# Recurrent layers of a four-stage block: the short convolution moved off TensorE, the clip folded into a product, output scalings gathered on ScalarE

## The chip, the cores and the metric

One core of a Trainium2 chip runs the whole program in one launch. The metric is the device time of one execution in microseconds (us), from runs on the chip. Engines are called as in the profile: PE (TensorE, matmul), PEld (its weight loads), DVE (VectorE), ACT (ScalarE), POOL (GpSimd), SP (SyncE).

## The reference

The block takes x of shape 8 x 512 x 256 in float32 and applies four sublayers, each followed by a residual addition and a layer norm: three gated recurrent layers, an expert layer in which experts choose tokens, an attention layer, and an expert layer in which tokens choose experts. The change lies in the recurrent layers alone:

```python
def _rglru_layer(x, cw, cb, wrw, wrb, wiw, wib, la, wow, nw):
    xp = jnp.pad(x, ((0, 0), (KCONV - 1, 0), (0, 0)))             # KCONV = 4
    x_conv = cb + sum((xp[:, k:k + Lx, :] * cw[:, k] for k in range(KCONV)))
    r_t = jax.nn.sigmoid(x_conv @ wrw.T + wrb)
    i_t = jax.nn.sigmoid(x_conv @ wiw.T + wib)
    a_base = jax.nn.sigmoid(la.astype(jnp.float32)).astype(x.dtype)
    a_t = a_base ** (8.0 * r_t)
    b_t = jnp.sqrt(jnp.clip(1.0 - a_t * a_t, 1e-06, None)) * (i_t * x_conv)
    h = _parallel_scan(a_t, b_t)
    return _rmsnorm(h @ wow.T, nw)
...
for l in range(NLAYERS):                                          # NLAYERS = 3
    h = _rglru_layer(h, conv_w[l], ...)
return _rmsnorm(h, norm_out_w)
```

## The kernel before

The 4096 tokens are cut into four groups of two sequences (1024 tokens). A *unit* u is one layer on one group: three layers times four groups make U = 12 units, u = 0 to 11, with the group index changing fastest. Channels lie on the 128 partitions, in two chunks (`dc` = 0, 1), and tokens along the free dimension, so a tile of a unit is 128 x 2 x 2 x 512 elements (chunk, sequence, time).

The work of a unit is software-pipelined over rounds t = -2 to 11. In round t the kernel convolves unit t+2 (`conv`, `taps`), forms the gates of unit t+1 (`gate`, `square_decay`), does the scans of unit t (`sums`, `decay`, `clip`, `root`, `gated`, `inputs`, `scan`), and projects, normalizes and transposes back unit t-1 (`project`, `norm`, `scaled`, `turn`). Rounds -2 to 8 are written in `usual`, rounds 9 to 11 in `late` (unit t-1 is then one of the last layer), and `end` finishes the last unit. PE, ACT and DVE run under a manual schedule: each executes its instructions in exactly the order in which these functions issue them. So an instruction that waits holds back all that was issued behind it on its engine.

The steps that the change and the prediction speak of:

- `conv(u, i)` (L252) starts the convolution. Where `on_pe(u, dc)` holds, PE multiplies with two diagonal matrices (L268 and L271, the tap of shift 0 and that of shift 1, half a chunk at a time) and ACT moves the sum from PSUM to the tile `xc` with the bias (L274). Elsewhere ACT forms the tap of shift 0 with the bias for a whole chunk at once (L261). Before, `on_pe` holds for chunk 0 of every unit and for both chunks of the last unit.
- `taps(u, dc)` (L278) adds the other shifts on DVE (L283): shifts 2 and 3 where PE took part, shifts 1, 2 and 3 elsewhere.
- `gate` (L288): PE multiplies `xc` with the two gate matrices (L296), ACT applies a tanh (L300) and writes `R` and `I`. `square_decay` (L304): ACT writes Q, the squared decay, from R.
- `sums(u, dc)` (L313) on DVE: a bounded sum of logarithms by scans, then differences, into `D`. `decay` (L329): ACT takes the exponential of `D`. `clip` (L335) on DVE turns Q into min(Q - 1, -1e-6). `root` (L339): ACT takes the square root of -Q/4. `gated` (L342) and `inputs` (L345) on DVE multiply I with `xc` and with that root; `scan` (L348) runs the recurrence on DVE into `h`, of which there is one buffer.
- `project` (L357): PE multiplies h with the output matrix (L369) into PSUM, ACT squares and sums each 256 wide row (L379). In the last layer DVE first multiplies by a weight (L375). `norm` (L394): a square root on ACT (L400, or L405 in the last layer), a reciprocal on DVE (L407). `scaled(u, c)` (L409) scales each of eight pieces: in the first two layers ACT does six (L418) and DVE those with c = 2 and 3 (L416), from PSUM into Y. `turn` (L420) transposes Y back on PE, and ACT writes `xT` (L430).

ACT's functions need tables: root and norm use another table than the exponentials and the tanh, so each round has two table loads. All PSUM tiles of these layers come from one pool of eight banks, in which a new tile takes the bank whose last use stands earliest in program order.

In a usual round ACT's order is: squares of two projections, `decay` of chunk 0, convolution, squares of the other two, table load, `root`, `norm`, `scaled`, table load, `decay` of chunk 1, R, Q, then I and `xT` in turn. DVE's order is: sums of chunk 0, `clip`, sums of chunk 1, `gated`, first tap of chunk 1, reciprocal, the other taps of chunk 1, `scaled`, `inputs`, taps of chunk 0, four scans.

Of the kernel before, what the change touches and what calls it, by code (L numbers as in the profile page):

```python
# [10 lines left out]
F32 = mybir.dt.float32  # L11
I32 = mybir.dt.int32
AF = mybir.ActivationFunctionType
ALU = mybir.AluOpType
# [3 lines left out]
P = 128  # L18
# [132 lines left out]
def recurrent_layers(tc, x_tok, xT, lg, ident, eps6, eps5, acc, kept, a):  # L151
# [5 lines left out]
    nc = tc.nc  # L157
# [4 lines left out]
    U = NL * NG  # L162
    with ExitStack() as ctx:
        wp = ctx.enter_context(tc.tile_pool(name="rw", reuse_waits="tile", bufs=1))
# [29 lines left out]
        nc.vector.memset(wg, 0.0)  # L194
        nc.scalar.dma_start(wg[:, :, :E0], a["Wg"].rearrange("(dc p) e -> p dc e", p=P))

        on_pe = lambda u, dc: dc == 0 or u == U - 1
        diag = {}
        for l in range(NL):
            for dc in range(DC):  # L200
# [17 lines left out]
        table = wp.tile([P, 1], F32, name="table")  # L218
        one = wp.tile([P, 1], F32, name="one1")
        nc.vector.memset(one, 1.0)  # L220
        eps12 = wp.tile([P, 1], F32, name="eps12")
        nc.vector.memset(eps12, RMS_EPS * RMS_EPS)

# [26 lines left out]
        xcs, Rs, Is, Qs, Cs, Ds, hs, Ys, ws, sss = ({} for _ in range(10))  # L250

        def conv(u, i):  # L252


            l, q = stages[u]
            dc, b = divmod(i, NB)
            if i == 0:
                xcs[u] = new("xc", u, 3)
            if not on_pe(u, dc):
                if b == 0:  # L260
                    nc.scalar.activation(  # L261
                        xcs[u][:, dc].rearrange("p b t -> p (b t)"), xT[:, dc, q * W : (q + 1) * W],
                        AF.Identity, bias=par[:, l, dc, CB : CB + 1], scale=par[:, l, dc, 3:4],
                    )
                return
            ps = psG.tile([P, S], F32, tag="g", name=f"conv_{u}_{i}")
            at = q * W + b * S
            nc.tensor.matmul(  # L268
                ps, diag[l, dc, 0], xT[:, dc, at : at + S], start=True, stop=False
            )  # L270
            nc.tensor.matmul(  # L271
                ps[:, 1:], diag[l, dc, 1], xT[:, dc, at : at + S - 1], start=False, stop=True
            )
            nc.scalar.activation(  # L274
                xcs[u][:, dc, b, :], ps, AF.Identity, bias=par[:, l, dc, CB : CB + 1]
            )

        def taps(u, dc, k=slice(None)):  # L278
            l, q = stages[u]
            src = xT[:, dc, q * W : (q + 1) * W].rearrange("p (b t) -> p b t", b=NB)  # L280
            dst = xcs[u][:, dc]
            for s in ((2, 3) if on_pe(u, dc) else (1, 2, 3))[k]:
                nc.vector.scalar_tensor_tensor(  # L283
                    dst[:, :, s:], src[:, :, : S - s], par[:, l, dc, 3 - s : 4 - s],
                    dst[:, :, s:], ALU.mult, ALU.add,
                )
# [26 lines left out]
        def sums(u, dc):  # L313

            l, q = stages[u]
            if dc == 0:
                Cs[u], Ds[u] = new("C", u, 1), new("D", u, 1)
            C, Df = Cs[u][:, dc], Ds[u][:, dc]
            nc.vector.tensor_scalar(
                Df, Rs[u][:, dc], 1.0, mlim[:, l, dc : dc + 1], ALU.add, ALU.min  # L320
            )
            for b in range(NB):
                nc.vector.tensor_tensor_scan(
                    C[:, b, :], Df[:, b, :], clim[:, l, dc : dc + 1].to_broadcast([P, S]),
                    0.0, ALU.add, ALU.min,
                )
            nc.vector.tensor_sub(Df[:, :, 1:], C[:, :, 1:], C[:, :, : S - 1])

        def decay(u, dc):  # L329
            l, q = stages[u]  # L330
            nc.scalar.activation(
                Ds[u][:, dc], Ds[u][:, dc], AF.Exp, scale=neg4[:, l, dc : dc + 1]
            )

        def clip(u):  # L335

            nc.vector.tensor_scalar(Qs[u], Qs[u], 1.0, -1e-6, ALU.subtract, ALU.min)

        def root(u):  # L339
            nc.scalar.activation(Qs[u], Qs[u], AF.Sqrt, scale=-0.25)  # L340

        def gated(u):  # L342
            nc.vector.scalar_tensor_tensor(Is[u], Is[u], 1.0, xcs[u], ALU.add, ALU.mult)

        def inputs(u):  # L345
            nc.vector.tensor_mul(Is[u], Is[u], Qs[u])

        def scan(u, dc):  # L348
            if dc == 0:
# [44 lines left out]
        def norm(u, c0=0, n=NCH, last=False):  # L394


            l, q = stages[u]
            s = sss[u][:, 0, c0 : c0 + n]
            if l < NL - 1:
                nc.scalar.activation(s, s, AF.Sqrt, bias=eps6, scale=1.0 / D)  # L400
            else:
                nc.vector.scalar_tensor_tensor(
                    s, s, RMS_EPS, sss[u][:, 1, c0 : c0 + n], ALU.mult, ALU.add
                )
                nc.scalar.activation(s, s, AF.Sqrt, bias=eps12, scale=1.0 / D)  # L405
            if not last:
                nc.vector.reciprocal(s, s)  # L407

        def scaled(u, c):  # L409
            l, q = stages[u]  # L410
            s = sss[u][:, 0, c : c + 1]
            dst, src = Ys[u][:, c, :], ws[u][c // 2][:, c % 2, :]
            if l == NL - 1:
                nc.vector.scalar_tensor_tensor(dst, dst, s, nob, ALU.mult, ALU.mult)
            elif c // 2 == 1:
                nc.vector.tensor_scalar_mul(dst, src, s)  # L416
            else:
                nc.scalar.mul(dst, src, s)  # L418

# [27 lines left out]
        def last_norm(u, c0, n):  # L447

            last_root(u, c0, n)
            last_scale(u, c0, n)  # L450
            last_apply(u, c0, n)
# [90 lines left out]
        def usual(t):  # L542
            A, G, R, O, N = on(t + 2), on(t + 1), on(t), on(t - 1), is_last(t - 2)
            if R:
                sums(t, 0)
                clip(t)
                sums(t, 1)
                gated(t)
            for i in range(4):
                if O:  # L550
                    project(t - 1, i)
                if R and i == 1:
                    decay(t, 0)
                if A and i == 1:
                    conv(t + 2, 0)
                    conv(t + 2, 2)
            if A:
                taps(t + 2, 1, slice(0, 1))
            if R:
                root(t)  # L560
            if O:
                norm(t - 1)
            if A:
                taps(t + 2, 1, slice(1, 3))
            if O:
                for c in range(NCH):
                    scaled(t - 1, c)
            if R:
                inputs(t)
            if A:  # L570
                conv(t + 2, 1)
                taps(t + 2, 0)
            if R:
                decay(t, 1)
                scan(t, 0)
                scan(t, 1)
            for i in range(4):
                if G:
                    gate(t + 1, 0, i)
            if G:  # L580
                square_decay(t + 1)
            for i in range(4):
                if G:
                    gate(t + 1, 1, i)
                if O:
                    turn(t - 1, i)

        def late(t):


            A, G, N = on(t + 2), on(t + 1), is_last(t - 2)
            sums(t, 0)
            for i in range(4):
                project(t - 1, i)
                if i == 1:
                    decay(t, 0)
                    if A:
                        conv(t + 2, 0)
                    clip(t)
            if is_last(t - 3):  # L600
                for b in range(NB):
                    logits(t - 3, b)
                take_logits(t - 3)
            sums(t, 1)
            decay(t, 1)
            gated(t)
            root(t)
            norm(t - 1)
            if N:
                last_norm(t - 2, 0, NCH)  # L610
                keep(t - 2, 0, NCH)
            inputs(t)
            if A:
                for i in range(1, 4):
                    conv(t + 2, i)
                taps(t + 2, 0)
            scan(t, 0)
            if A:
                taps(t + 2, 1)
            scan(t, 1)  # L620
            for c in range(NCH):
                scaled(t - 1, c)
            if G:
                for i in range(4):
                    gate(t + 1, 0, i)
                square_decay(t + 1)
            for b in range(NB):
                residual(t - 1, b)
            for i in range(4):
                if G:  # L630
                    gate(t + 1, 1, i)
                if N:
                    last_turn(t - 2, i)
# [50 lines left out]
        for t in range(-2, U):  # L684
            (late if is_last(t - 1) else usual)(t)
# [1610 lines left out]
```

## Time and profile before

| what | value |
|---|---|
| median of 3 runs | 1828.58 us (1828.22 to 1832.04) |
| profiled execution, its own time | 1832.25 us |
| its span in the profile | 1830.5 us |
| mean granted TensorE clock | 0.968 of full |
| busy: PE, DVE, ACT, POOL | 1683.4, 1135.8, 972.1, 510.8 us |
| first sums of round 1 start at | 58.08 us |
| eight rounds, 1 to 8 | 58.08 to 265.50 us |
| three late rounds, 9 to 11 | 265.50 to 369.6 us |
| end of the recurrent layers and last logits | to about 403 us |
| everything else | 403 to 1830.5 us |

Times inside the program are from the span's start. "Busy" adds up an engine's instructions, of which neighbours may overlap by about 0.1 us; the ends of matmuls are modelled. A line number is that of the kernel before unless the text says otherwise. A line of the timeline gives start, duration, engine, source line, operation, output <- inputs, shapes and count; the bracket says how long the engine was idle before and whose result ended the idle time. The stretches are cut at the first DVE instruction of a round (L319).

### The profile page before, as it was taken

To read this page: it belongs to the slowest core of one execution; us is meant where nothing else is said; L and a number is where in the kernel's file an instruction comes from. 1 tells how busy PE (TensorE), PEld (TensorE's weight loads), DVE (VectorE), ACT (ScalarE), POOL (GpSimd) and SP (SyncE) were. 2 spreads that over 40 slices of the span, in tenths; PEclk is the share of its full clock that TensorE was granted. 3 is DMA by queue.
4 is the path that set the end of the run, shared out by engine and by line. 5 is a ranking of instruction groups with operands and counts; after the bars stand their busy time and mean duration, and the time that the engine had idled before them with its cause. 6 is when DMAs were issued, how large, how long until landed. Compare 5 with 4: busy or idle time off the path is not lost. (4 is left out here: it accounts for less than half of the span.)

```text
span 1830.5 us, 31418 instructions
## 1 busy us (share of the span) xinstructions
PE 1683.4 (92%) x10280; PEld 1104.9 (60%) x10280; DVE 1135.8 (62%) x2846; ACT 972.1 (53%) x2128; POOL 510.8 (28%) x464
## 2 busy tenths in 40 slices
PE   6999997567999799999999999988999999999995
PEld 2555663346999575222222232226999889999984
DVE  5999998787222644687978888785453222222227
ACT  4899986631232423566666665656454343343333
POOL 1000000000554410010242341424667644444440
PEclk8999999679999899999999999999999999999998
DMA  9200000032451400000011120125766678575548
GB/s 356 75 1 0 1 1 1 23 127 102 125 169 59 121 6 7 18 18 16 27 57 40 40 68 18 62 78 162 176 161 146 145 193 218 102 166 119 98 90 265
DMA packets 108424, 167.30 MB, mean 91 GB/s; under 512 B 16669, under 2 KB 83807, under 8 KB 108000
## 3 DMA queue, kind: packets, MB, share of 16 engines
q1 hardware_dynamic: 76064, 117.74, 20.3%
q0 software_dynamic: 29184, 44.85, 12.7%
q10 hardware_dynamic: 3008, 2.63, 0.4%
q8 instruction: 86, 1.41, 0.3%
q14 instruction: 82, 0.67, 0.1%
HBM read 232.75 MB, written 60.07 MB: 160 GB/s over the span
## 5 line engine op out<-in xcount | busy, mean ns | idle before, releaser
L2053 DVE TENSOR_REDUCE nmx<-s 128x1 f32<-128x512 f32 x512 | 329.8, 686 | 100.9 <-PE t L1972 76.7
L2060 ACT ACTIVATE pe<-t 128x512 f32<-128x512 f32 x512 | 277.5, 595 | 187.5 <-PE t L1972 178.4
L1957 PE MATMUL s<-kT,qT 32*128 32x512 f32 x1024 | 289.5, 640 | 24.4 <-DVE nmx L2053 13.8
L1972 PE MATMUL t<-qA,kT 32*128 32x512 f32 x1024 | 285.1, 641 | 0.3 <-DVE nmx L2053 0.3
L2149 POOL DMA_INDIRECT acc<-y,at x136 | 211.4, 1554 | 240.8 <-DVE at L2142 165.0
L1957 PEld LDWEIGHTS s<-kT,qT 32*128 32x128 f32 x1024 | 78.7, 183 | 171.7 <-ACT pe L2060 158.3
L972 ACT ACTIVATE m1hT<-m1h,m1ws 128x128 f32<-128x128 f32 x272 | 99.3, 368 | 152.1 <-PE m1h L966 114.2
L2148 DVE TENSOR_SCALAR y<-m1o,gt 128x256 f32<-128x256 f32 x136 | 65.8, 484 | 174.4 <-PE m1o L988 163.9
L972 ACT ACTIVATE m1hT<-m1h,xT 128x128 f32<-128x128 f32 x272 | 98.5, 368 | 135.3 <-PE m1h L966 103.3
L955 DVE COPY m1xq<-m1xp 128x256 f32<-128x256 f32 x136 | 57.7, 424 | 168.2 <-PE m1h L966 108.0
L735 POOL DMA_INDIRECT m1rows<-x_ext,slot x128 | 128.4, 1003 | 97.6 <-ACT pe L2060 64.1
L1996 PE MATMUL po<-pe,V 128*17 128x512 f32 x1024 | 135.1, 600 | 1.4 <-ACT pe L2060 1.0
L966 PEld LDWEIGHTS m1h<-m1xq,m1ws 128*128 128x128 f32 x1088 | 133.0, 194 | 3.7 <-issue 0.5
L966 PE MATMUL m1h<-m1xq,m1ws 128*128 128x128 f32 x1088 | 134.5, 277 | 0.0
L966 PEld LDWEIGHTS m1h<-m1xq,xT 128*128 128x128 f32 x1088 | 131.5, 192 | 4.8 <-DVE m1xq L955 0.9
L966 PE MATMUL m1h<-m1xq,xT 128*128 128x128 f32 x1088 | 132.9, 275 | 0.8 <-DVE m1xq L955 0.7
L988 PE MATMUL m1o<-m1ws,m1hT 128*128 128x256 f32 x544 | 129.3, 381 | 0.6 <-issue 0.6
L988 PE MATMUL m1o<-xT,m1hT 128*128 128x256 f32 x544 | 128.7, 379 | 0.0
L2026 POOL TENSOR_TENSOR AO<-AO,on 128x256 f32<-128x256 f32 x32 | 23.6, 737 | 349.2 <-DVE on L2021 235.6
L988 PEld LDWEIGHTS m1o<-m1ws,m1hT 128*128 128x128 f32 x544 | 98.6, 191 | 11.6 <-issue 1.0
L988 PEld LDWEIGHTS m1o<-xT,m1hT 128*128 128x128 f32 x544 | 98.1, 190 | 10.5
L296 PE MATMUL gate<-xc,wi 128*128 128x512 f32 x192 | 92.1, 611 | 2.5 <-ACT junk L379 2.5
(367 smaller groups left out, 2925.3 us busy)
## 6 DMA issues: line engine op xcount, KB each, us to landing
m1ws<-in_w_pack SPq DMA_DIRECT2D x68, 522.0 KB
m1ws<-in_w_pack SPq DMA_DIRECT2D x68, 512.0 KB
xT<-in_w_pack SPq DMA_DIRECT2D x66, 522.0 KB
xT<-in_w_pack SPq DMA_DIRECT2D x66, 512.0 KB
m0ws<-in_w_pack SPq DMA_DIRECT2D x36, 522.0 KB
m1xg<-m1rows SPq DMA_DIRECT2D x136, 138.0 KB
m0ws<-in_w_pack SPq DMA_DIRECT2D x36, 512.0 KB
acc<-zero SPq DMA_DIRECT2D x2, 4096.0 KB
```

The source lines that it names most:

```text
L296: nc.tensor.matmul(ps, w[("wr", "wi")[g]][:, l, dc, oc * P : (oc + 1) * P], xcs[u][:, dc, b, :], start=(dc == 0), stop=(dc == DC - 1),)
L735: ins = self.nc.gpsimd.indirect_dma_start(out=self.rows[:, :], out_offset=bass.IndirectOffsetOnAxis(ap=place, axis=0), in_=row, in_offset= ...
L966: nc.tensor.matmul(ps, w[:, o : o + P], xq[:, dc, :], start=(dc == 0), stop=(dc == DC - 1),)
L972: ins = nc.scalar.activation(hT[:, fc, :], ps, AF.Gelu, bias=w[:, o : o + 1])
L988: nc.tensor.matmul(ps, hT[:, fc, :], w[:, o : o + D], start=(fc == 0), stop=(fc == FC - 1))
L1957: mm = nc.tensor.matmul(ps, qTs[u % NR][r, qc * P : (qc + 1) * P], kTs[u % NR][r, :], start=True, stop=True,)
L1972: mm = nc.tensor.matmul(ps, kTs[v % NR][r, kc * P : (kc + 1) * P], qAs[v][r, :], start=True, stop=True,)
L1996: mm = nc.tensor.matmul(po[h4 * HP : h4 * HP + VW, :], V[:, b * NQ + kc, 4 * g + h4, :], pes.pop((u, kc, h4)), start=(kc == 0), stop=(kc = ...
L2053: ins = nc.vector.tensor_reduce(at, ps, AX.X, ALU.max, negate=True)
L2060: ins = nc.scalar.activation(pe, ps, AF.Exp)
L2148: nc.vector.tensor_scalar_mul(y, ps, gt)
L2149: nc.gpsimd.indirect_dma_start(out=R.acc[t % 2][:, :], out_offset=bass.IndirectOffsetOnAxis(ap=at, axis=0), in_=y, in_offset=None, compute ...
```

## The change

Three edits. First, `on_pe` holds for the last unit only: in the eleven units before it ACT forms the first tap of both chunks, one instruction for each, and DVE adds three shifts for both. Half of the diagonal matrices are no longer built on POOL (L205), since only those of the last layer are used. Second, `clip` is gone: the root takes sqrt(1/4 + 2^-24 - Q/4) with a bias tensor, and the product that follows takes the larger of the root and half of sqrt(1e-6) in the same instruction. Third, `scaled` is done on ACT for all eight pieces in the first two layers. The order of calls in `usual`, `late` and `end` is otherwise unchanged.

```diff
-        on_pe = lambda u, dc: dc == 0 or u == U - 1
+        on_pe = lambda u, dc: u == U - 1
...
+        quarter = wp.tile([P, 1], F32, name="quarter")
+        nc.vector.memset(quarter, 0.25 + 2.0**-24)
...
-        def clip(u):
-
-            nc.vector.tensor_scalar(Qs[u], Qs[u], 1.0, -1e-6, ALU.subtract, ALU.min)
-
         def root(u):
-            nc.scalar.activation(Qs[u], Qs[u], AF.Sqrt, scale=-0.25)
+
+            nc.scalar.activation(Qs[u], Qs[u], AF.Sqrt, bias=quarter, scale=-0.25)
...
         def inputs(u):
-            nc.vector.tensor_mul(Is[u], Is[u], Qs[u])
+            nc.vector.scalar_tensor_tensor(
+                Is[u], Qs[u], 0.5 * math.sqrt(1e-6), Is[u], ALU.max, ALU.mult
+            )
...
             if l == NL - 1:
                 nc.vector.scalar_tensor_tensor(dst, dst, s, nob, ALU.mult, ALU.mult)
-            elif c // 2 == 1:
-                nc.vector.tensor_scalar_mul(dst, src, s)
             else:
                 nc.scalar.mul(dst, src, s)
...
                 sums(t, 0)
-                clip(t)
                 sums(t, 1)
...
                     if A:
                         conv(t + 2, 0)
-                    clip(t)
```

## The prediction

> **What bounds the kernel now.** The change touches only the recurrent layers, so the first view is the busy time by stretch, cut at DVE's first L319 of each round (columns: stretch, us, then busy us and instructions of PE, PEld, DVE, ACT, POOL, then clock, DMA share, GB/s). The startup runs to 58.08, eight equal rounds to 265.50, then three rounds of another kind and the end.
>
> ```profile
> 58.08:84.00 25.92, 25.92 (x90) 15.33 (x89) 25.61 (x23) 22.55 (x43) 0.00 (x0) 1.00 0.00 1
> ...
> 161.79:187.72 25.93, 25.93 (x90) 15.32 (x90) 25.61 (x24) 23.88 (x46) 0.00 (x0) 1.00 0.00 1
> ...
> 303.70:336.70 33.00, 22.22 (x64) 11.56 (x63) 30.39 (x52) 26.20 (x61) 1.12 (x37) 0.79 0.09 33
> ```
>
> A round takes 25.93, and PE and DVE are both full in it; ACT has some 2 us left. So relief of PE alone buys nothing: DVE must get shorter too, and its waits must not grow. The second view is the timeline of one round, DVE and then ACT (start, us, engine, line, what; in brackets the idle time before).
>
> ```profile
> 161.79 0.75 DVE L319 TENSOR_SCALAR D<-R,mlim 128x1024 f32<-128x1024 f32 x1
> ...
> 166.09 1.22 DVE L337 TENSOR_SCALAR Q<-Q 128x2048 f32<-128x2048 f32 x1
> 167.23 0.75 DVE L319 TENSOR_SCALAR D<-R,mlim 128x1024 f32<-128x1024 f32 x1
> ...
> 174.92 0.20 DVE L407 RECIPROCAL ss<-ss 128x8 f32<-128x8 f32 x1
> ...
> 177.56 0.87 DVE L416 TENSOR_SCALAR Y<-wo,ss 128x256 f32<-128x256 f32 x2
> 178.34 2.28 DVE L346 TENSOR_TENSOR I<-I,Q 128x2048 f32<-128x2048 f32 x1
> 180.54 2.59 DVE L283 SCALAR_TENSOR_TENSOR xc<-xT,par,xc 128x1020 f32<-128x1020 f32 x2
> 183.05 4.56 DVE L352 TENSOR_TENSOR_SCAN h<-D,I 128x512 f32<-128x512 f32 x4
> 187.72 0.75 DVE L319 TENSOR_SCALAR D<-R,mlim 128x1024 f32<-128x1024 f32 x1
> ```
>
> ```profile
> 166.21 1.15 ACT L331 ACTIVATE D<-D,neg 128x1024 f32<-128x1024 f32 x1 [0.27 <-DVE D L327]
> 167.27 0.67 ACT L274 ACTIVATE xc<-conv,par 128x512 f32<-128x512 f32 x1
> 167.84 1.23 ACT L261 ACTIVATE xc<-xT,par 128x1024 f32<-128x1024 f32 x1
> 168.97 0.37 ACT L379 ACTIVATE junk<-wo 128x256 f32<-128x256 f32 x1
> ...
> 171.13 1.28 ACT L340 ACT_TABLE_LOAD   x1
> 172.42 1.91 ACT L340 ACTIVATE Q<-Q 128x2048 f32<-128x2048 f32 x1
> 174.24 0.28 ACT L400 ACTIVATE ss<-ss,eps 128x8 f32<-128x8 f32 x1
> ```
>
> The reader is to see a loop through both engines. ACT's decay waits for DVE's first sums (+4.42 from the round's start); behind it in ACT's queue stand the convolution, four squares, the table load, the root and the norm; DVE's reciprocal needs that norm. The norm ends at 174.52 and DVE takes it at 174.92: a margin of 0.40, so DVE never waits.
>
> **The change in the eight rounds.** Costs are start-to-start distances, since neighbours overlap by about 0.1. DVE loses the clip (166.09 to 167.23: 1.14) and two scalings (177.56 to 178.34: 0.78). It gains the first tap of chunk 0: three taps took 3.82 in round 0 (44.88 to 48.70), two take 2.51 (180.54 to 183.05), so 1.31. The product becomes the two-operator form; the nearest row is L343, the same width, 2285 ns against 2279: nothing. DVE's own work is 25.93 - 1.14 - 0.78 + 1.31 = 25.32, and DVE reaches the reciprocal at 13.13 - 1.14 = 11.99.
>
> ACT, from the decay at +4.42: decay 1.06 to the next start, then two convolutions of 1.13 (L261 to L379) where one of 0.57 and one of 1.13 stood. The first square starts at 7.74. The squares and their reads took 2.16 to the table load, of which 0.59 was delay for PE's projection; PE no longer has a convolution between the projections, so that goes: 1.57, table load at 9.31, root at 10.60. Root gets a bias tensor; L308 with two pointer operands takes 1248 ns, L331 with one 1149, so I take 0.10 (bounds 0 and 0.10): 1.92. Norm from 12.52 to 12.80; the reciprocal follows at 0.04, as it did in round 10 (320.47, 320.51): 12.84. DVE, ready at 11.99, now waits 0.85. The round is 25.32 + 0.85 = 26.17, 0.24 longer; eight rounds: **+1.9**. Each term is good to 0.02 or so, the wait to 0.15, so the eight give 0.5 to 3.0. Queued behind the waiting reciprocal are the rest of DVE's round and, on ACT, the output scalings.
>
> The two scalings given to ACT cost 2 x 0.36 (six take 2.16, 175.15 to 177.31). They stand after the reciprocal, where an eviction of 0.74 (177.31 to 178.05) goes; the second decay starts at 17.4 as before (17.55), the scan that needs it starts near 23.8. Hidden; without that cover 0.7 a round. "ScalarE: Activation LUTs" of the Trainium skill, Rules for kernel authors, speaks against this edit: a plain multiply belongs on VectorE, up to about three times as fast in bf16. The trace differs for this fp32 tile read from PSUM: 0.39 apart on DVE, 0.36 on ACT; three times as slow would be an estimated 1.4 us more on ACT per round.
>
> PE loses eight passes (3.44 a round, 164.84 to 166.56 and 170.01 to 171.72) and waits instead, about 1.1 for the third scan, 1.0 and 0.9 for evictions of PSUM banks. The clock bears on that, read in stretches of its own 3.41 us step: after 2.16 us or more of PE work in a stretch it stayed full, after 1.71 or less it was half in the next.
>
> ```profile
> 292.68:296.10 3.42, 2.30 (x11) 1.96 (x11) 3.42 (x7) 0.44 (x1) 0.00 (x0) 1.00 0.00 0
> ...
> 306.34:309.75 3.41, 1.18 (x3) 0.19 (x1) 3.38 (x5) 1.04 (x6) 0.00 (x0) 1.00 0.00 0
> 309.75:313.16 3.41, 3.17 (x4) 1.17 (x4) 3.38 (x5) 3.41 (x16) 0.00 (x0) 0.50 0.00 0
> ```
>
> A stretch after the change holds one gap, so 2.3 us of work at least: the clock stays. "TensorE: Matmul & The Clock Gate" (Part 1, and its table "Why this matters for your kernels") asks for an idle window, gaps above about 3 us, before the rate halves; here 1.18 us of work in the window was too little. By that rule there would be no danger at all.
>
> **The change in the startup.** Round 0 and its lead-in have nothing to hide a tap or a convolution. ACT ends its DMA issues at 13.03. Now the exponential at 14.32 is followed by the convolution of chunk 0 (1.23) before the next table load (1.28): the logarithm starts at 17.05 instead of 15.85, the convolution of chunk 1 ends at 18.48, DVE's small operations (1.16 after the logarithm) end at 18.54. Taps start there, 0.66 later than the 17.88 of the trace. Three take 3.84, so unit 0 is complete at 26.2 and the first gates start at 26.39 instead of 24.40; unit 1's taps end at 33.91, and the sums start then instead of at 31.54. They take 8.60 without the clip: 42.51. The gated product needs the last I of the first gates, 41.81 + 1.99 = 43.80: it starts at 43.84. ACT issues decay and two convolutions behind that I (43.69, 44.74, 45.87 to 47.10), so DVE's next tap waits until 47.13. Then 3.84 + 2.20 + 3.84 + 4.67 (taps, product, taps, scans): 61.68, against 58.08: **+3.6**. How long PE runs at half clock from 26.39 is open: some 5 us in the trace, 3.4 to 6.8 by the position of the step; half of the difference moves the last I, so 2.6 to 4.3.
>
> **The late rounds.** The clip goes (1.14 of DVE), but the reciprocal waits 2.34 for ACT in each (L407, "2.34 <-ACT ss L405"), and ACT is busy from the first L379 to the second decay at 315.93, only 0.12 after it is free. So 0.1 back in rounds 9 and 10 against 0.10 for root in each: **+0.1** in all, bounds -0.4 and +0.3. The fewer diagonal matrices on POOL are nothing: it idles there.
>
> **Sum.** 3.6 + 1.9 + 0.1 = +5.6. What follows, from 403 us, starts from the last logits and shifts whole. On the profiled execution, 1832.25 (span 1830.5 and 1.75 around it), that is 1837.85; that execution was 3.67 above the median, so against 1828.58 I say **1834.2**. The runs shown lie 3.8 us apart; about 0.2%, or 3.7 us, is the least that can be told from no change, up to 1832.2.
>
> **Rivals.** *DVE alone sets the rounds.* If ACT's norm is done by 11.99, the wait of 0.85 does not appear, a round is 25.32, and eight give -4.9: with 3.6 and 0.1 that is -1.2, 1827.4, not slower. It decides only where ACT's chain is 0.85 shorter than its rows. For it: DVE's list really is shorter. Against: all eight rounds agree to 0.02, and the decay's start is fixed by DVE itself. *PE goes cold in its gaps.* One half-rate step costs 1.7 of PE work; the fourth projection would be ready at 6.3 and is needed at 8.5, so that is hidden. Two steps in a round cost 3.4, less 2.2 of margin: 1.2 a round, 9.6 in all, 1843.8. Against it stand the 2.3 us above. *PE was the real bound.* Then relief of 3.44 a round would bring up to 27 us, but DVE's 25.32 caps that: it becomes the first rival.
>
> **How the numbers follow.** My case 0.83, with a range of 1831.3 to 1836.2 (1828.58 and the lower or the upper bounds of the three terms: 0.5 to 3.0, 2.6 to 4.3, -0.4 to 0.3); DVE alone 0.12; cold PE 0.05. For eight in ten the ends are widened towards the rivals by part of the 3.8 between the runs shown: 1829 to 1837.5. Slower by over 0.2%: 0.64 of my case and the 0.05, 0.69. Same: 0.19 of mine and 0.06 of the first rival, 0.25. Faster: 0.06, the rest of that rival.
>
> **What would show it** (lines of the changed kernel). Right: a wait of DVE at the reciprocal for ACT's L401 near 0.85 in each of eight rounds; rounds of 26.17; the first L321 at 33.9 and the second round at 61.7; PE waiting 3 us or more a round at full clock. Wrong: no such wait; rounds of 25.3; a granted clock of 0.5 inside the rounds; a startup within 1 us of before; late rounds shorter by 1.

## The result, and the profile after

The changed kernel is slower: 1844.23 us median (1837.40 to 1845.87) beside 1832.69 (1828.22 to 1837.11) for the kernel before on the same chip, a ratio of 1.006 [1.0042, 1.0077]. That is 11.5 us; the forecast was +5.6, to 1834.2 within 1829.0 to 1837.5. The direction was right, the size half of what came. In absolute time the forecast missed by 10.0: 5.9 of that is the change, and 4.1 is the start, for 1828.58 was a median of three runs and the kernel before now took 1832.69. A later comparison of the same two kernels gave 1.0056 [1.0037, 1.0076].

The profiled execution after took 1838.37, its span is 1836.6. It lies 5.9 below the median of its version, so its profile shows 6.1 of the 11.5. The same stretches as before (stretch, us, busy us and instructions of PE, PEld, DVE, ACT, POOL, clock, DMA share, GB/s), cut at the first DVE L321 of rounds 1, 5 and 10:

```profile
60.58:86.89 26.31, 25.14 (x82) 14.82 (x81) 25.00 (x21) 22.91 (x44) 0.00 (x0) 0.94 0.00 1
165.19:191.29 26.10, 23.45 (x81) 13.61 (x80) 25.01 (x21) 24.45 (x47) 0.00 (x0) 1.00 0.00 1
307.56:340.52 32.96, 20.49 (x64) 10.97 (x63) 29.22 (x51) 26.20 (x61) 1.12 (x37) 0.84 0.09 33
```

A usual round is 26.10 instead of 25.93. PE is now idle for 2.65 of it (the forecast had 3.0) and DVE, shorter of work, is not full either. The timeline of round 5, DVE and then ACT, shows where DVE stands:

```profile
165.19 0.76 DVE L321 TENSOR_SCALAR D<-R,mlim 128x1024 f32<-128x1024 f32 x1
...
175.99 1.28 DVE L285 SCALAR_TENSOR_TENSOR xc<-xT,par,xc 128x1022 f32<-128x1022 f32 x1
178.01 0.20 DVE L408 RECIPROCAL ss<-ss 128x8 f32<-128x8 f32 x1 [0.74 <-ACT ss L401]
178.13 2.54 DVE L285 SCALAR_TENSOR_TENSOR xc<-xT,par,xc 128x1020 f32<-128x1020 f32 x2
180.59 2.28 DVE L345 SCALAR_TENSOR_TENSOR I<-Q,I 128x2048 f32<-128x2048 f32 x1
182.79 3.91 DVE L285 SCALAR_TENSOR_TENSOR xc<-xT,par,xc 128x1022 f32<-128x1022 f32 x3
186.62 4.57 DVE L353 TENSOR_TENSOR_SCAN h<-D,I 128x512 f32<-128x512 f32 x4
191.29 0.75 DVE L321 TENSOR_SCALAR D<-R,mlim 128x1024 f32<-128x1024 f32 x1
```

```profile
169.61 1.15 ACT L333 ACTIVATE D<-D,neg 128x1024 f32<-128x1024 f32 x1 [1.32 <-DVE D L329]
170.67 2.36 ACT L263 ACTIVATE xc<-xT,par 128x1024 f32<-128x1024 f32 x2
172.93 0.36 ACT L380 ACTIVATE junk<-wo 128x256 f32<-128x256 f32 x1
...
174.49 1.28 ACT L339 ACT_TABLE_LOAD   x1
175.78 2.00 ACT L339 ACTIVATE Q<-Q,quarter 128x2048 f32<-128x2048 f32 x1
177.69 0.28 ACT L401 ACTIVATE ss<-ss,eps 128x8 f32<-128x8 f32 x1
```

This is the forecast's loop: two convolutions of 1.13 ahead of the squares put ACT's norm at +12.50, and DVE waits for it.

The rest of the loss lies behind the recurrent layers. Shifts of DVE's markers against the first profile of before:

| marker | before, us | after |
|---|---|---|
| first sums, round 0 | 31.54 | +2.48 |
| round 1 | 58.08 | +2.50 |
| round 9 | 265.50 | +4.08 |
| last logits | 401.55 | +4.95 |
| copy of `pt`, routing of the first expert layer | 406.22 | +9.68 |
| first transposed rows of that layer | 456.47 | +10.02 |
| attention, at 1107 us | 1107.46 | +10.07 |
| last maximum of the attention | 1227.43 | +6.43 |
| end of span | 1830.5 | +6.1 |

Between the last logits and the copy of `pt` another 4.7 us go. The timeline of SP's queue and of PE's filler products in that stretch, before. (Filler products are matmuls whose result nobody reads, issued to keep PE busy; each shows as two in the trace. Here they read `blk`, a mask that SP loads.)

```profile
389.63 7.29 SPq L486 DMA_DIRECT2D kept<-x_ext  x3
396.97 1.04 SPq L1757 DMA_DIRECT2D wq<-in_Wq  x1
398.06 1.25 SPq L1757 DMA_DIRECT2D wk<-in_Wk  x1
399.42 0.49 SPq L1379 DMA_DIRECT2D blk<-in_c_blk  x1
...
403.40 3.75 SPq L1792 DMA_DIRECT2D bt<-in_bt  x8
...
403.04 2.92 PE L1200 MATMUL idle<-blk,ident 128*128 128x128 f32 x24 [1.53 <-DMA blk<-in_c_blk]
```

and after:

```profile
50.63 1.23 SPq L1754 DMA_DIRECT2D wq<-in_Wq  x1
...
393.56 6.92 SPq L485 DMA_DIRECT2D kept<-x_ext  x3
400.57 6.74 SPq L1789 DMA_DIRECT2D bt<-in_bt  x3
407.37 0.42 SPq L1376 DMA_DIRECT2D blk<-in_c_blk  x1
...
410.44 5.19 PE L1197 MATMUL idle<-blk,ident 128*128 128x128 f32 x24 [3.98 <-DMA blk<-in_c_blk]
```

The diff names no DMA here, yet the queue has another order: `wq` and `wk` (and `wv`) have gone to the startup, and three loads of `bt` (tables for the attention) now stand ahead of `blk`. PE waits 3.98 for `blk` instead of 1.53 and runs its 24 filler products, at half clock, in 5.19 instead of 2.92: 2.45 + 2.27 = 4.72, the whole jump. The transpose that makes `pt` is queued behind them. The longer wait is the queue's; the half clock is not the queue's alone. In this profile it had stood since 398.2, before the wait. Over all profiles with this mask the 24 products took 4.54 to 5.46 in the seven with the changed order, but also 5.37 to 5.46 in four of the nine with the old one, and 2.92 in the other five.

The 3.6 that come back in the attention are no gain of the change. In before's first profile the clock stood at half from 1180.2 to 1183.6; a second profile of before has no such step and is 3.8 shorter there.

### The profile page after: what moved, and what is told of

Read it like the earlier page. It is cut to its first block, busy times and chain, and to the rows that moved or that the text cites. A ratio compares the mean times of both kernels' runs of the same rounds, so it can differ in the third digit from the quotient of the medians.

```text
span 1836.6 us, 31226 instructions
## 1 busy us (share of the span) xinstructions
PE 1651.3 (90%) x10192; PEld 1088.9 (59%) x10192; DVE 1128.5 (61%) x2830; ACT 977.0 (53%) x2133; POOL 507.7 (28%) x460
## 5 line engine op out<-in xcount | busy, mean ns | idle before, releaser
L298 PE MATMUL gate<-xc,wr 128*128 128x512 f32 x192 | 85.9, 601 | 26.6 <-DVE xc L285 26.6
L985 PEld LDWEIGHTS m1o<-m1ws,m1hT 128*128 128x128 f32 x544 | 98.3, 191 | 11.5 <-issue 1.0
```

What stands on the lines that cost most here:

```text
L298: nc.tensor.matmul(ps, w[("wr", "wi")[g]][:, l, dc, oc * P : (oc + 1) * P], xcs[u][:, dc, b, :], start=(dc == 0), stop=(dc == DC - 1),)
L985: nc.tensor.matmul(ps, hT[:, fc, :], w[:, o : o + D], start=(fc == 0), stop=(fc == FC - 1))
```

## The experiments

Theory after the first look: the recurrent layers cost about 5 us by the forecast's mechanism, and the new order of SP's queue about 4.7; the matrices no longer built free 2 KB a partition, and SP's order depends on where tiles lie. Rivals: the jump is chance (a clock step), or it belongs to PE's state after the layers. The first four ran beside 35 executions of before, median 1832.98.

**Four spare tiles** in place of the matrices:

```diff
+        for k in range(4):
+            pad = wp.tile([P, P if k else P - 8], F32, name=f"pad{k}")
+            nc.gpsimd.memset(pad[:, 0:1], 0.0)
```

> The changed kernel with four unused tiles that fill the 2 KB per partition which the missing diagonal matrices left free, so that every later tile lies where it lay before. Theory A (the shorter list of tiles moves later tiles, the attention weights' loads no longer wait for the recurrent layers, and two loads for the attention layer come ahead of the block mask in SP's queue; the mask is late and PE's products on it hold back the router's transposes): SP's order is that of before, the 5.5 us between the last logits and the router's first transposes go, and the kernel is 3.5 to 4.5 us above before (ratio 1.002). Theory B (PE's clock happens to be low there, whatever the queue): the 5.5 us stay, 9 to 11 above before.

1839.86, 1.004 [1.0021, 1.0059]: 6.9 above before, more than the 3.5 to 4.5 expected. SP's queue stands as before, and PE waits 1.36 for `blk`. So four tiles that hold nothing turn the order back. The profiled execution nevertheless lost several us behind the layers, to half clock (below).

**Filler products that need no load:**

```diff
-    idle_products(nc, psR, ident, blk, 12)
+    idle_products(nc, psR, ident, ident, 12)
```

> The changed kernel, in which the twelve filler products before the router's transposes multiply the identity instead of the block mask, so that PE does not wait for the mask there; SP's order stays as in the changed kernel, the mask is next needed some 7 us later. Theory A: PE's wait of 3.98 for the mask goes and the transposes follow the probabilities at once; 4 to 5.5 us less than the changed kernel, 4 to 5.5 above before. Theory B: nothing changes, 9 to 11 above before.

1840.87, 1.0048 [1.0032, 1.0064]; the jump at `pt` is gone (+5.17 at the last logits, +4.55 at the copy). The time is 7.9 above before, not 4 to 5.5.

**The kernel before with the diagonal matrices in shared buffers**, built when needed; nothing else of the change:

```diff
+        def diagonals(l, dc):
+            for s in range(2):
+                diag[l, dc, s] = wp.tile([P, P], F32, tag=f"diag{s}", bufs=2, name=f"diag{l}_{dc}_{s}")
...
+            if on_pe(u, dc) and (l, dc, 0) not in diag:
+                diagonals(l, dc)
```

> The kernel before, its arithmetic and its order on PE, ACT and DVE unchanged, with the diagonal matrices of layers 0 and 2 (and 1 and 2) sharing buffers and those of layer 2 built on POOL just before they are needed: 2 KB per partition less, as in the changed kernel. Theory A: SP's order becomes that of the changed kernel, the jump of 5 to 6 us appears between the last logits and the router's transposes, the recurrent layers take as long as before: 5 to 6 us above before (ratio 1.003). Theory B, or the blame on the convolution: 0.

1835.08, 1.0018 [0.9997, 1.0038]; its queue has the changed order, and its trace has the jump: +0.21 at the last logits, +3.77 at the copy. In the time, where 5 to 6 us were expected, this comparison does not tell it from no change; the third quiet pair below does.

**The convolution of chunk 0 later on ACT**, behind the output scalings and just ahead of its taps (with the spare tiles; the tile `xc` is then made by whichever convolution comes first):

```diff
...
-                    conv(t + 2, 0)
                     conv(t + 2, 2)
...
-                conv(t + 2, 1)
+                conv(t + 2, 0)
                 taps(t + 2, 0)
```

> As e1_pad, with the convolution of chunk 0 issued on ACT after the output scalings instead of between the squares, just ahead of the taps that need it. Theory of the loop (decay, two convolutions, squares, table load, root and norm on ACT stand between DVE's first sums and its reciprocal): the norm ends 1.13 earlier, DVE's wait of 0.74 at the reciprocal goes, a round takes 25.3 to 25.4 instead of 26.10; eight rounds give 5.8 back: 2 us below before (ratio 0.999). Rival: ACT is the bound with 24.5 us busy, DVE waits at the first tap of chunk 0 or at the second decay instead, rounds stay near 26.1 and the time equals e1_pad.

1827.66, 0.9979 [0.9959, 0.9998], faster than before. One round, and DVE at the reciprocal:

```profile
158.38:183.71 25.33, 23.19 (x82) 13.69 (x81) 24.98 (x22) 24.45 (x47) 0.00 (x0) 1.00 0.00 1
```

```profile
169.18 1.28 DVE L289 SCALAR_TENSOR_TENSOR xc<-xT,par,xc 128x1022 f32<-128x1022 f32 x1
170.37 0.20 DVE L412 RECIPROCAL ss<-ss 128x8 f32<-128x8 f32 x1
```

No idle time stands at the reciprocal: the wait belonged to the convolution's place in ACT's queue. What is left, 25.33, is the sum of DVE's own work that the forecast had as 25.32. Its startup cost is gone too (+0.16 at the first sums, -1.02 at round 1).

The next four ran beside 35 executions of before, median 1833.42.

> The changed kernel once more, unaltered, beside the kernels below on one chip. Theory: its extra time has two parts, the recurrent layers (+4 to +5 us, as the four spare tiles' version showed: 1.004) and the reordered queue of SP (+2.4 to +4.7), so the ratio to before is 1.0035 to 1.0055 and it stands 3 to 5 us above the version with four spare tiles. Rival: the reordered queue costs nothing on average, and the first comparison's 1.006 was the scatter of clock steps between executions: ratio 1.004 or less. In its profile the copy of pt should again come some 4.7 us later, against the last logits, than before.

1844.54, 1.0056 [1.0037, 1.0076]. The jump at `pt` came again: +6.22 at the last logits, +9.86 at the copy.

**The late convolution without the spare tiles:**

> The changed kernel with the convolution of chunk 0 issued late on ACT, just before its taps, but without the four spare tiles, so that SP's queue stands in the changed order. The same version with the spare tiles measured 0.9979. Theory (queue order costs 2.4 to 4.7 us): ratio 0.9992 to 1.0005, and pt copied about 4 us later against the last logits than in the version with the spare tiles. Rival (order costs nothing): 0.998 again, and no such delay.

1833.63, 0.9999 [0.9981, 1.0017]: the queue's order takes the gain back. PE waits 3.41 for `blk` here against 1.46 with the spare tiles, and the copy of `pt` comes 4.0 later.

**The late convolution with the spare tiles and four more filler products** ahead of the inversion of the routing (64 small products on PE in the first expert layer):

```diff
-            idle_products(nc, psX, ident, pt, 15)
+            idle_products(nc, psX, ident, pt, 19)
```

> The late convolution with the four spare tiles, and 19 instead of 15 filler products on PE ahead of the products that invert the routing (L1403). In two of six profiles PE fell to half clock there for 27 us, where a gap of 2.08 us lay inside one clock step of 3.41; in the others the gap was cut by a step's edge and the clock stayed. Theory (cold steps are what makes executions of one kernel differ): four more products, 1.8 us, close the gap, no half clock between the routing sums and the inversion, 5.2 us less in those executions that fell into it, so 1 to 2 us less in the mean than the same version with 15 (0.9979): about 0.997. Rival: the extra products delay the inversion instead, up to 1.8 us more: 0.999.

1826.10 (1822.88 to 1828.61), 0.9961 [0.9943, 0.9979], the fastest version; the same with 15 ranged from 1822.95 to 1834.90. What the fillers prevent, in the change with spare tiles (stretches of one clock step each, then PE's timeline):

```profile
447.58:450.99 3.41, 1.33 (x9) 0.93 (x8) 3.38 (x4) 2.60 (x12) 0.00 (x0) 1.00 0.56 169
450.99:454.41 3.42, 3.42 (x18) 3.42 (x18) 3.38 (x5) 3.22 (x16) 0.00 (x0) 0.50 0.99 332
```

```profile
441.72 6.64 PE L1201 MATMUL idle<-pt,ident 128*128 128x256 f32 x30
450.44 13.40 PE L1136 MATMUL inverse<-of,lane 128*128 128x80 f32 x64 [2.08 <-DVE lane L1132]
```

and the same lines of its twin with 19 (further below):

```profile
438.52 8.37 PE L1201 MATMUL idle<-pt,ident 128*128 128x256 f32 x38
447.23 7.64 PE L1136 MATMUL inverse<-of,lane 128*128 128x80 f32 x64 [0.34 <-DVE lane L1132]
```

A gap of 2.08 inside one step of 3.41 leaves 1.33 of work; the clock halves at its end and the inversion takes 13.40 instead of 7.64; in two more profiles whose gap lies inside a step it takes 13.26 and 13.51. In seven other profiles with such a gap (1.99 to 2.09) an edge of the clock's steps cuts it, and the inversion takes 7.63 or 7.64. In the second profile of the change an edge cuts it too, and yet the clock halves and the inversion takes 11.87:

```profile
452.41:455.83 3.42, 2.25 (x20) 2.28 (x21) 3.39 (x4) 3.16 (x16) 0.00 (x0) 1.00 0.86 315
455.83:459.24 3.41, 3.41 (x18) 3.41 (x18) 2.60 (x3) 3.39 (x16) 0.00 (x0) 0.50 0.96 353
```

So the cut helps mostly, not always.

**Clip and scalings alone**, the convolution left on PE:

```diff
-        on_pe = lambda u, dc: u == U - 1
+        on_pe = lambda u, dc: dc == 0 or u == U - 1
```

> The clip folded into the product and all output scalings on ACT, but the convolution of chunk 0 left on PE as before, so that DVE loses 1.92 us a round and gains nothing. Theory (the loop through DVE's reciprocal and ACT's norm sets the round where PE has room): DVE's own work 24.01, ACT's norm at 12.83 against DVE's arrival at 11.99, a wait of 0.88 and rounds of 24.89: 8 x -1.04 = -8.3 us, ratio 0.9955, startup about -1. Rival (PE, shown as busy for 25.92 of 25.93 before, is a real bound of its own): rounds stay at 25.9 and the ratio is 0.9995 to 1.0005; DVE then waits about 1.9 a round for results of PE.

1831.67, 0.9987 [0.9969, 1.0006]. A round, and DVE at the reciprocal in the round before it:

```profile
159.74:185.57 25.83, 25.83 (x89) 15.24 (x88) 23.72 (x21) 24.60 (x49) 0.00 (x0) 1.00 0.00 1
```

```profile
147.78 0.20 DVE L408 RECIPROCAL ss<-ss 128x8 f32<-128x8 f32 x1 [1.78 <-ACT ss L401]
```

There ACT's squares wait for PE:

```profile
143.40 0.39 ACT L380 ACTIVATE junk<-wo 128x256 f32<-128x256 f32 x1 [0.86 <-PE wo L370]
```

The theory of 24.89 a round was wrong here and its rival right. DVE gave up 1.92 a round and 0.10 of it reached the round: PE, without a gap in all 25.83, is the bound, and holds DVE through those squares. So before, PE and DVE stood within 0.10 of each other.

The last two groups ran beside before at 1829.49 and 1829.38.

**The convolution alone**, clip and scalings as before, with spare tiles:

> The convolution off PE alone: chunk 0 on ACT and DVE in eleven units, with the clip kept on DVE and the output scalings shared as before, and four spare tiles that keep SP's queue in the order of before. Theory (DVE and ACT form the loop, PE only gains room): DVE's own work 25.93 + 1.31 = 27.24, DVE reaches the reciprocal at 13.13 and ACT's norm is done at 12.70, so no wait, rounds of 27.24: 8 x 1.31 = +10.5 us, and 2.5 to 4 in the startup: ratio 1.007 to 1.008. Rival (the second convolution on ACT is what costs, through the wait at the reciprocal, and DVE has room for a tap): rounds of 26.1 as in the whole change, a wait of 0.7 in each, ratio 1.0025 to 1.0035.

1850.95, 1.0091 [1.0061, 1.0122]. Rounds 1 to 8 take 27.24 each, to 0.01, with no wait at the reciprocal; round 9 starts 12.66 late. The third tap costs 1.31 a round as worked out, where nothing else leaves DVE.

**Before, and the change with spare tiles, each with 19 fillers:**

> The kernel before with 19 instead of 15 filler products ahead of the inversion of the routing, nothing else. Theory (cold steps of the clock in that gap are part of every version's scatter, 5.2 us in the executions that fall into it): mean 1 to 3 us lower, ratio 0.9985 to 0.9995, and its slowest executions, near 1841, gone. Rival (the filler helped only the version with the late convolution, by its alignment): ratio 1.000 and the same spread of 15 us.

1829.52 (1827.72 to 1831.68), 0.9989 [0.9975, 1.0004] (ratios here are not quotients of the two medians): the spread falls from 12.6 to 4.0, the median does not move, since 16 of the 23 executions of before lay below 1830.3 here.

> The whole change with the four spare tiles and with 19 filler products: queue order as in before and the gap of the clock closed, so that only the recurrent layers differ from the kernel before with 19 fillers. Theory: it stands 4.6 to 5.2 us above that kernel (the shift of the last logits in the traces so far), ratio to before 1.0015 to 1.0025. Rival (the 2 to 3 us that the version with spare tiles stood above its recurrent layers' shift come from something else behind them, not from the clock): 7 to 8 us above, ratio 1.003 to 1.004.

1836.58, 1.0028 [1.0014, 1.0043]: 7.1 above its twin, which is the rival's 7 to 8, and in the ratio just below its 1.003. In the two traces 4.07 are there at the last logits, 4.46 at 456, 7.30 at 626; the last 2.8 are a half clock of 13.6 us against 6.8, in PE's wait for the first expert rows.

> The kernel before once more, for a second profile of it. Theory: its recurrent layers end within 0.3 us of the first profile; the differences of several us lie where the clock's steps of 3.41 us fall otherwise: the half-rate step at 1180 us, worth 3.8 us in the first profile, is absent, or the gap near 450 us is cold for some 20 us more. Rival: its stretches agree with the first profile to 1 us throughout, and the scatter between executions lies outside the profiled span.

1829.66. It agrees to 0.5 us up to 457, loses 3.0 in that same wait (half clock for 13.7 us instead of 6.8), and is 3.8 shorter at 1180. Between these two profiles the difference is the clock's. Nor is the longer half clock in that wait the change's own: of the thirteen profiles in which the inversion ran at full clock, nine have 6.8 us of it there and four 10.2 to 13.7, three of those with the rounds of before. How often each version meets it is open.

**The three pairs again, now quiet:** each with 19 fillers and SP's queue in the changed order.

> The whole change with 19 filler products and without the spare tiles: SP's queue in the changed order. With the old order it measured 1.0028. Theory (the order costs 3.6 to 4.7 us): 1.0048 to 1.0054. Rival (the order costs nothing on average, the fillers already hide it): 1.0028 within its interval.

> The late convolution with 19 filler products and without the spare tiles. With the old order it measured 0.9961. Theory: 0.9981 to 0.9987. Rival: 0.996.

> The kernel before with its diagonal matrices in shared buffers (the footprint, and so SP's order, of the changed kernel) and 19 filler products. With the old order it measured 0.9989. Theory: 1.0009 to 1.0015. Rival: 0.999.

| version, 19 fillers | old order | changed order |
|---|---|---|
| the whole change | 1.0028 [1.0014, 1.0043] | 1.0053 [1.0038, 1.0067] |
| late convolution | 0.9961 [0.9943, 0.9979] | 1.0004 [0.9994, 1.0014] |
| the kernel before | 0.9989 [0.9975, 1.0004] | 1.0022 [1.0010, 1.0034] |

All three stand higher, by 0.0025, 0.0043 and 0.0033 or 4.6, 7.9 and 6.0 us; the intervals are apart in the second and third. The ratios carry the scatter of before, whose median was 1833.42 beside one of these versions and 1829.4 or 1829.5 beside the others; the versions' own medians, taken on different chips, stand 2.9, 4.7 and 5.8 apart. The theory had 3.6 to 4.7. PE's fillers in the third pair, old order and then changed:

```profile
402.45 2.92 PE L1200 MATMUL idle<-blk,ident 128*128 128x128 f32 x24 [1.46 <-DMA blk<-in_c_blk]
```

```profile
405.54 4.62 PE L1207 MATMUL idle<-blk,ident 128*128 128x128 f32 x24 [3.74 <-DMA blk<-in_c_blk]
```

## Why the prediction was half right

- **The steps that failed** are "The fewer diagonal matrices on POOL are nothing" and, built on it, "What follows, from 403 us, starts from the last logits and shifts whole". POOL did idle, but without the matrices' four tiles SP's loads, far behind the layers, are queued otherwise. That is shown both ways: spare tiles restore the order, smaller buffers in the kernel before make it change. That it comes from the room the tiles take, which sets where later tiles lie, is argued: both edits also change four early POOL instructions (in the spare tiles, memsets of one column), and which tile then overlaps which was not tested. Price: 4.7 in the profile, 4.6 to 7.9 by the ratios of the quiet pairs and 2.9 to 5.8 by their medians, against 0 forecast.
- **DVE's own work and the third tap**: 25.32 and 1.31 forecast; 25.33 in the late version and 27.24 - 25.93 with the convolution alone.
- **The wait**: 0.74 in seven rounds and 0.96 in the first, for 0.85; ACT's norm ended at +12.78 for +12.80. The round is 26.10 for 26.17, so eight gave +1.58 for +1.9.
- **The clock in PE's gaps**: full in seven rounds of the profile, half for 3.4 us in the first (26.31; 27.50 in the second profile of the change, with 6.8 us of it). "The clock stays" held for the steady rounds and not for the first, and not for the reason given. "2.3 us of work at least" in every stretch was wrong: steady rounds of the change have steps with 1.90 (125.09 to 128.50), between the 1.71 that had halved the clock and the 2.16 that had kept it. That they stayed full was luck for the forecast.
- **The startup**, 3.6 forecast with bounds 2.6 to 4.3: 2.50 in the profile, just outside. First sums at 34.02 for 33.91, but PE ran less long at half clock, the last I ended at 42.72 for 43.80, and the gated product at 42.75 for 43.84. Other profiles of the change's rounds gave 2.5 to 3.9 at round 1: the bounds were nearly right, the centre a little high.
- **Late rounds**: -0.2 for +0.1. The waits at the reciprocal grew (3.46 in round 10) by about what the clip had cost.
- **The sum to the last logits**: these terms give 3.9 in the profile, and +3.6 stand just before the last logits. Another 1.4 comes in these, where the clock stood at half from 398.2 on and each sixteen products took 1.08 instead of 0.64; the forecast had no such term. So 4.95 (3.6 to 6.2 in six profiles of the change's rounds) for 5.6: that half stands.
- **The rivals**: DVE alone set the rounds once the convolution was issued late, not in the change. PE as a real bound was dismissed too lightly: it lay 0.10 behind DVE, which is why clip and scalings alone gave nothing. The price of the cold PE, 1843.8, lies near the measured 1844.23 by chance: it was built from two half steps in each round, and the profile has one in eight rounds.

In the quiet pairs the whole change costs 1.0053 against 0.9989, 0.0064 or 11.7 us (10.0 between the medians). Their two traces have 9.8 of it: +5.2 at the last logits, +10.1 at the copy of `pt`, +9.8 at the end, so in them the recurrent layers and the jump are the whole cost. In the old order 7.1 remain, 4.1 of them in the recurrent layers; of the other 3, behind them, 2.8 are the half clock in the wait for the expert rows, and how usual that is stays open as said above.

## What to carry to other kernels

When an edit removes tiles, compare the order of every queue that a scheduler fills, to the end of the program, and not only the engines that the edit touches; four dead tiles were worth 3 to 8 us here. In a loop of in-order engines, place new work behind the instruction that another engine waits for: the same convolution, moved some instructions down ACT's queue, turned 1.004 into 0.998. And relieving two engines that bound together pays only when both are relieved.

## What the runs showed of the hardware

The clock's steps of 3.41 us lie anywhere against the program: counted from the start of the span, their edges stood from 0.29 to 3.19 us past a multiple of 3.41 in the seventeen profiles. The same gap of 2.08 us therefore cost nothing in the profile of before (the inversion took 7.63) and 5.8 in that of the change with spare tiles (13.40), and 35 executions of before spread over 15 us. Four filler products cut the spread of before from 12.6 to 4.0. The Trainium skill, "TensorE: Matmul & The Clock Gate" (Part 1), also has a free-running window of 3413 ns; it lets the clock drop after an idle window, while here one with 1.33 us of work was enough.

How much work keeps the clock up, PE's busy time in a step does not tell alone. The forecast's two bounds, from one profile, do not hold over all: with clip and scalings alone, a step with 1.42 us of work kept full clock, and the step with 2.25 shown above lost it.

```profile
440.81:444.22 3.41, 1.42 (x7) 0.91 (x5) 3.34 (x11) 1.97 (x9) 0.00 (x0) 1.00 0.34 86
444.22:447.64 3.42, 3.35 (x30) 3.38 (x31) 3.39 (x4) 3.23 (x16) 0.00 (x0) 1.00 1.01 370
```

The 1.42 are filler products 256 columns wide, the 2.25 the inversion's, 80 wide; whether width counts was not tested.
